# Where the zeros of a graph layer's score table stand in the DMA queue: behind the first value weights, and tied to the last stores of both projections

## The chip, the cores and the metric

The kernel runs on one core of one Trainium2 chip. The metric is the device time of one execution in microseconds. The median of three runs is compared.

## What is computed

The kernel computes two layers over a graph of 625 nodes with 1024 features and 10,000 edges. The change lies in the first of them, which adds two things to x: a graph attention (GATv2) and a linear attention. Cut to what matters:

```python
x = xn * rsqrt(mean(xn**2) + eps) * rms_w            # xn: layer norm of the input
x = x @ W_down                                       # 1024 -> 256
xl, xr = x @ Wl, x @ Wr                              # left and right projection, 625 x 256
msg = xl[src] + xr[dst]                              # one row for each edge (and each self loop)
e = einsum('ehd,hd->eh', leaky_relu(msg), att)       # 4 scores for each edge
p = exp(e - max over dst)                            # softmax over the edges of a destination
out = segment_sum(p / denom * xl[src], dst) @ W_up
# beside it, from the same xn, linear attention with 16 heads:
k, v, q = phi(xn @ W_k + b_k), xn @ W_v + b_v, phi(xn @ W_q + b_q)
```

Then come a quantised feed-forward block, a second layer of graph convolution and linear attention, and an attention with a mixture of eight experts. They take most of the time and are not touched.

## The kernel before, in words

The nodes are tiled as 5 tiles of 125 rows. In the first stage each tile is loaded, normalised (`norm`), transposed (`turn_x`), multiplied by W_down (`down`) and by both projections at once (`left_right`, lines 541 to 551). The result of `left_right` is in SBUF in `xlr`; its left half is stored to the DRAM tensor `xl_d` from ScalarE's queue and its right half to `xr_d` from GpSimd's queue, by the helper `rows_dma` (lines 171 to 174). That helper makes two DMAs of each tile, of 112 and of 13 rows.

The edges are worked on by gathers. 79 chunks of up to 128 edges are grouped by two. For each chunk GpSimd gathers rows of `xl_d` and of `xr_d` (`gather`, line 611), VectorE adds and weighs them into four scores (`score_group`, `score`, lines 586 to 594 and 621), ScalarE takes the exponential into `es`, and GpSimd scatters the result into `table` in DRAM (`scatter`, line 631). `table` has an entry of four values for each pair of nodes, source by destination, and is 128 * 3080 entries of 16 bytes, 6160 KB. An entry without an edge must be zero, so the table is filled with zeros by one DMA from the small tile `none` (line 404) before anything is scattered into it. The scores of the self loops (`own`) go into the table's diagonal from ScalarE's queue (`self_loops`).

Meanwhile TensorE computes the linear attention: `key` and `value` for each tile (`pk` and `pv` in the profile, 16 matmul records each), and between them the counts of the edges by one-hot matmuls (`pct`, line 467, operands in `ring`). After that come `query` and `answer` (`pq`, `pd`, `po`) and the output projection (`mixed`, line 745).

The order in which each engine takes its work is the order in which the program writes it down, in this stage by hand: `manual_schedule` fixes the order of TensorE, VectorE, ScalarE, GpSimd and SyncE. `Stream` (`do`) issues the work of one step's TensorE part and, one step later, the part that evacuates its result. `work(us)` adds planned time to a counter, and when it has passed a threshold, `one_beat` puts one group of edges into the queues: the self loops if due, the scores of an earlier group, its exponentials, then its gathers and the scatters of a still earlier one. The first gather of a group (a beat) is held back until the latest matmul group written down before it is done:

```python
if j == 0 and side == 0 and "pe" in latest:
    behind(got, latest["pe"])
```

`behind(ins, name)` makes one instruction wait for another by a semaphore; nothing else of it runs.

SyncE's queue holds the large loads in this order: the tiles of x with W_down, the projections' weights, the biases of the linear attention, the first key weights (`lin.wk`, two DMAs of 1024 KB, a `Half`), the zeros, the first value weights (`lin.wv`, two DMAs of 1024 KB), and after those the biases and weights of the linear attention's second half. An instruction that waits holds up all that stand behind it in the same engine's queue.

When all scatters are done, GpSimd loads the table back in five parts (`load_table`, `tb`), VectorE multiplies it by the counts (`weigh`, `pT`, line 841), and TensorE sums it (`sums`, `pg`).

Of the kernel before, what the change touches and what calls it, by code (L numbers as in the profile page):

```python
# [20 lines left out]
NT = 5  # L21
P = 125
# [20 lines left out]
def gps_kernel(tc: tile.TileContext, w: dict, out: bass.AP):  # L43

    again = attempt(tc, w, out, False)
    with tc.If(again > 0):
        attempt(tc, w, out, True)  # L50
# [3 lines left out]
def attempt(ctx: ExitStack, tc: tile.TileContext, w: dict, out: bass.AP, shifted: bool):  # L54

    nc = tc.nc
# [6 lines left out]
    def ps1(name):  # L63
        pool, n = psums[-1]
        return pool.tile([128, 512], FP, tag="ps1", name=name, bufs=n)
# [61 lines left out]
    def group(dst, pairs):  # L127

        for i, (lhsT, rhs) in enumerate(pairs):
            made = nc.tensor.matmul(dst, lhsT=lhsT, rhs=rhs, start=(i == 0), stop=(i == len(pairs) - 1))  # L130
        latest["pe"] = made.ins.name
# [3 lines left out]
    def behind(ins, name):  # L135

        tc.add_manual_dep(ins.ins, name, mybir.DependencyInfo(mybir.DependencyClass.Sync,
                                                              mybir.DependencyReason.DATA), reason="pace")
        return ins
# [30 lines left out]

    def rows_dma(eng, dst, src):

        eng.dma_start(out=dst[0:112], in_=src[0:112])
        eng.dma_start(out=dst[112:P], in_=src[112:P])


    graph = ctx.enter_context(ExitStack())
# [41 lines left out]
    def mid(shape, name):  # L219
        return midp.tile(shape, FP, tag="mid", name=name)  # L220
# [135 lines left out]
    with ExitStack() as st0:  # L356
# [4 lines left out]
        table = dram.tile([128 * 3080, 4], FP, name="table")  # L361
# [3 lines left out]
        with ExitStack() as edges:  # L365
# [4 lines left out]

            xin = big.tile([P, NT, D], FP, tag="big", name="xin")
            rows_dma(nc.sync, xin[:, 0, :], xrows[0])

            si = pool.tile([128, EN], I32, name="si")
            di = pool.tile([128, EN], I32, name="di")
            rw = pool.tile([128, KC], FP, name="rw")
            nc.scalar.dma_start(out=rw, in_=w["rms_w"])
            rows_dma(nc.sync, xin[:, 1, :], xrows[1])
            wd = wpool.tile([128, KC, 256], FP, tag="w", name="wd")
            nc.sync.dma_start(out=wd, in_=w["W_down"].rearrange("(k p) n -> p k n", p=128))  # L380
            for t in range(2, NT):
                rows_dma(nc.sync, xin[:, t, :], xrows[t])
# [5 lines left out]
            def load_edges():  # L388
                for dst, name in ((si, "src"), (di, "dst")):
# [8 lines left out]
            none = pool.tile([128, 440], FP, name="none")  # L398
# [2 lines left out]
                                  lambda us: work(us), nc.sync)  # L401
            lin.biases(0)
            lin.wk = Half(wpool, w["L0_Wk"], 0)
            nc.sync.dma_start(out=table.rearrange("(p a b) h -> p a (b h)", p=128, a=28),
                              in_=none.unsqueeze(1).to_broadcast([128, 28, 440]))
            lin.wv = Half(wpool, w["L0_Wv"], 0)
            sf = pool.tile([128, EN], FP, name="sf")
            df = pool.tile([128, EN], FP, name="df")
            up = pool.tile([128, EN], FP, name="up")
# [88 lines left out]
            xlr = mid([P, NT, 512], "xlr")  # L498
            xl_d = dram.tile([N, 256], FP, name="xl_d")
            xr_d = dram.tile([N, 256], FP, name="xr_d")  # L500
# [39 lines left out]
            def left_right(t):  # L540
                def pe():
                    hold["pl", t] = ps1("plr")
                    xdT = hold.pop(("xdT", t))
                    group(hold["pl", t][:P], [(xdT[:, k, :], wlr[:, k, :]) for k in range(2)])

                def after():
                    nc.scalar.activation(xlr[:, t, :], hold.pop(("pl", t))[:P], AF.Identity, scale=r0[:, t:t + 1])
                    rows_dma(nc.scalar, xl_d.rearrange("(t p) e -> t p e", p=P)[t], xlr[:, t, 0:256])
                    rows_dma(nc.gpsimd, xr_d.rearrange("(t p) e -> t p e", p=P)[t], xlr[:, t, 256:512])

                do(None, pe, after)

# [235 lines left out]
            for m in range(KC):  # L788
# [5 lines left out]
                if m < 3:  # L794
# [3 lines left out]
                                      in_=w[("w_gate", "w_up", "w_down")[m]].rearrange("(k p) n -> p k n", p=128))  # L798
# [418 lines left out]
    for m in range(KC):  # L1217
# [8 lines left out]
        a = m % 4  # L1226
# [48 lines left out]
    for b in range(NB_MIN, NB):  # L1275
        nc.gpsimd.dma_start(out=y_d[b * 128:(b + 1) * 128, :].rearrange("p (a n) -> p a n", a=4),
                            in_=zero.unsqueeze(1).to_broadcast([128, 4, 256]))
# [694 lines left out]
```

## Time and profile before

| what | value |
| --- | --- |
| median of 3 runs | 2227.58 us (2226.61 to 2228.72) |
| profiled execution, its own time | 2228.76 us |
| its span, first to last instruction | 2227.0 us |
| mean granted TensorE clock | 0.977 |
| bytes moved by DMA | 301.62 MB, mean 135 GB/s |
| zeros, one DMA | 6160 KB |

A line of a timeline has the start in us, the duration in us, the engine (a q behind it: its queue, an instruction that only issues), the source line, the operation, out<-in by the program's names, the shape, xcount, and in square brackets the idle time of the engine before it with what ended it. "issue" there means that the profile shows nothing it waited for, "remote" that the release came from an event with no instruction beside it in the profile. PE is TensorE, PEld its weight loads, DVE VectorE, ACT ScalarE, POOL GpSimd, SP SyncE. L611 is line 611 of the kernel before.

### The profile page before, as it was taken

How to read it: one execution, taken by the hardware profiler on the slowest of the kernel's cores; microseconds unless marked ns; L12 is line 12 of the kernel's file. 1: busy time of each engine (PE TensorE's matmuls, PEld its weight loads, DVE VectorE, ACT ScalarE, POOL GpSimd, SP SyncE). 2: the span in 40 equal slices, each digit the busy share in tenths (PEclk: the TensorE clock that was granted, in tenths of full speed). 3: DMA queues.
4: the chain of work that ended last, by engine and by line, in shares of the span. 5: the costliest groups of instructions: out<-in, count | busy, mean ns of one | idle time of the engine just before them, and what ended most of it. 6: DMA issues, size and time to landing. Idle time of an engine off the chain costs nothing. (4 is left out here: it accounts for less than half of the span.)

```text
span 2227.0 us, 17363 instructions
## 1 busy us (share of the span) xinstructions
PE 2112.5 (95%) x6934; PEld 1209.9 (54%) x6934; DVE 713.3 (32%) x1214; ACT 194.1 (9%) x354; POOL 341.4 (15%) x349
## 2 busy tenths in 40 slices
PE   8899799578899999999999999999999999999998
PEld 6466375245444777754445767557744444444443
DVE  5765467557623560000113133322011111111112
ACT  2000010001211100000000111100000000000000
POOL 1666656610000020210000000110000000000011
PEclk9999899878999999999999999999999999999999
DMA  9226252071122110231213111021099987997742
GB/s 299 77 62 209 59 182 81 25 212 33 38 85 71 52 38 1 85 142 38 76 38 104 38 38 38 20 103 61 34 347 337 331 325 282 327 331 286 275 144 92
DMA packets 145848, 301.62 MB, mean 135 GB/s; under 512 B 12370, under 2 KB 22436, under 8 KB 145754
## 3 DMA queue, kind: packets, MB, share of 16 engines
q1 hardware_dynamic: 123700, 244.23, 30.7%
q0 software_dynamic: 17376, 46.42, 7.1%
q10 hardware_dynamic: 4678, 9.72, 1.4%
q8 instruction: 58, 0.95, 0.2%
q14 instruction: 36, 0.29, 0.0%
HBM read 277.49 MB, written 22.84 MB: 135 GB/s over the span
## 5 line engine op out<-in xcount | busy, mean ns | idle before, releaser
L130 PE MATMUL pu<-w,xgT 128*128 128x512 f32 x768 | 333.9, 593 | 1.9 <-DVE xgT L1266 1.9
L130 PEld LDWEIGHTS pu<-w,xgT 128*128 128x128 f32 x768 | 144.0, 190 | 174.8 <-issue 171.7
L130 PE MATMUL pyb<-w,hb 128*128 128x512 f32 x384 | 174.3, 599 | 2.5 <-ACT yb L105 2.1
L130 PE MATMUL pq<-xnT,w 128*128 128x313 f32 x512 | 139.6, 432 | 13.8 <-DVE v L286 13.0
L130 PE MATMUL pk<-w,xnT 128*125 128x512 f32 x320 | 143.2, 599 | 3.3 <-issue 2.8
L130 PE MATMUL pv<-w,xnT 128*125 128x512 f32 x320 | 142.2, 597 | 1.5 <-issue 1.1
L130 PE MATMUL p<-tT,w 128*128 128x313 f32 x512 | 136.3, 428 | 0.4 <-DVE tT L1266 0.4
L130 PEld LDWEIGHTS pq<-xnT,w 128*128 128x128 f32 x512 | 98.2, 193 | 53.5 <-DVE v L286 13.8
L130 PEld LDWEIGHTS pyb<-w,hb 128*128 128x128 f32 x384 | 69.8, 189 | 90.9 <-issue 74.8
L1806 DVE TENSOR_TENSOR su<-pu,su 128x512 f32<-128x512 f32 x24 | 16.6, 692 | 314.6 <-ACT su L1805 314.6
L130 PEld LDWEIGHTS p<-tT,w 128*128 128x128 f32 x512 | 96.8, 190 | 37.9 <-issue 1.2
L130 PEld LDWEIGHTS pk<-w,xnT 128*125 128x125 f32 x320 | 59.8, 189 | 77.0 <-issue 76.1
L130 PEld LDWEIGHTS pv<-w,xnT 128*125 128x125 f32 x320 | 59.9, 189 | 75.4 <-issue 72.6
L1789 POOL DMA_INDIRECT xg<-rows_d,slots x12 | 11.4, 946 | 524.8 <-PE pxg L1796 449.0
L631 POOL DMA_INDIRECT table<-es,at x79 | 84.2, 1066 | 49.4 <-issue 26.2
L611 POOL DMA_INDIRECT ga<-xl_d,si x79 | 79.7, 1009 | 74.8 <-issue 33.2
L611 POOL DMA_INDIRECT gb<-xr_d,di x79 | 81.8, 1036 | 25.3 <-issue 22.8
L745 PE MATMUL px<-w,oT 128*125 128x512 f32 x160 | 69.8, 594 | 2.9 <-DVE x L909 2.0
L130 PE MATMUL px<-w,hT 128*125 128x512 f32 x160 | 70.3, 592 | 0.0
L130 PE MATMUL px<-w,oT 128*125 128x512 f32 x160 | 70.3, 592 | 0.0
L130 PE MATMUL ph<-meanT,w 128*128 128x313 f32 x256 | 70.1, 426 | 0.0
L130 PE MATMUL ph<-xnT,w 128*128 128x313 f32 x256 | 70.0, 427 | 0.0
(366 smaller groups left out, 2459.9 us busy)
## 6 DMA issues: line engine op xcount, KB each, us to landing
w<-in_eW_dram SPq DMA_DIRECT2D x144, 1024.0 KB
w<-in_L_Wk_dram SPq DMA_DIRECT2D x8, 1024.0 KB
w<-in_L_Wv_dram SPq DMA_DIRECT2D x8, 1024.0 KB
w<-in_L_Wq_dram SPq DMA_DIRECT2D x8, 1024.0 KB
w<-in_L_Wo_dram SPq DMA_DIRECT2D x8, 1024.0 KB
w<-in_W_self_dram SPq DMA_DIRECT2D x8, 1024.0 KB
w<-in_W_neigh_dram SPq DMA_DIRECT2D x8, 1024.0 KB
w<-in_sW_dram SPq DMA_DIRECT2D x8, 1024.0 KB
```

The costliest lines, as they stand in the source:

```text
L130: made = nc.tensor.matmul(dst, lhsT=lhsT, rhs=rhs, start=(i == 0), stop=(i == len(pairs) - 1))
L611: got = nc.gpsimd.indirect_dma_start(out=ab[g][side][0:p, j, :], out_offset=None, in_=src[:, :], in_offset=bass.IndirectOffsetOnAxis(ap=ix ...
L631: nc.gpsimd.indirect_dma_start(out=table[:, :], out_offset=bass.IndirectOffsetOnAxis(ap=at[0:p, lo + j:lo + j + 1], axis=0), in_=es[0:p, l ...
L745: made = nc.tensor.matmul(hold["px", t][:P, c, :], lhsT=oT[:, k, nodes(t)], rhs=wo[c](k), start=(k == 0), stop=(k == KC - 1 and keep is no ...
L1789: nc.gpsimd.indirect_dma_start(out=xg, out_offset=None, in_=rows_d[:, :], in_offset=bass.IndirectOffsetOnAxis(ap=slots[:, b:b + 1], axis=0))
L1806: nc.vector.tensor_tensor(su, pu[:, 0, :], su, op=ALU.mult)
```

## The change

The zeros' DMA is written down after the two DMAs of the first value weights instead of ahead of them, on the same queue. In addition it now waits for four stores: the two pieces of the last tile's left projection (`xl_d`) and the two of its right projection (`xr_d`). For that, `rows_dma` returns the DMAs that it makes. Nothing else moves: every other instruction keeps its place on its engine, and only the semaphores that the DMAs use are dealt out anew.

```diff
     def rows_dma(eng, dst, src):
-        eng.dma_start(out=dst[0:112], in_=src[0:112])
-        eng.dma_start(out=dst[112:P], in_=src[112:P])
+        return [eng.dma_start(out=dst[lo:hi], in_=src[lo:hi]) for lo, hi in ((0, 112), (112, P))]
...
             lin.wk = Half(wpool, w["L0_Wk"], 0)
-            nc.sync.dma_start(out=table.rearrange("(p a b) h -> p a (b h)", p=128, a=28),
-                              in_=none.unsqueeze(1).to_broadcast([128, 28, 440]))
             lin.wv = Half(wpool, w["L0_Wv"], 0)
+            zeros = nc.sync.dma_start(out=table.rearrange("(p a b) h -> p a (b h)", p=128, a=28),
+                                      in_=none.unsqueeze(1).to_broadcast([128, 28, 440]))
...
                     nc.scalar.activation(xlr[:, t, :], hold.pop(("pl", t))[:P], AF.Identity, scale=r0[:, t:t + 1])
-                    rows_dma(nc.scalar, xl_d.rearrange("(t p) e -> t p e", p=P)[t], xlr[:, t, 0:256])
-                    rows_dma(nc.gpsimd, xr_d.rearrange("(t p) e -> t p e", p=P)[t], xlr[:, t, 256:512])
+                    for put in (rows_dma(nc.scalar, xl_d.rearrange("(t p) e -> t p e", p=P)[t], xlr[:, t, 0:256])
+                                + rows_dma(nc.gpsimd, xr_d.rearrange("(t p) e -> t p e", p=P)[t],
+                                           xlr[:, t, 256:512])):
+                        if t == NT - 1:
+                            behind(zeros, put.ins.name)
```

## The prediction

> **What bounds the kernel now.** I read the page first, then the timelines of each engine from 0 to 140 us, where the change lies, then the waits up to 460 us, then the timelines again around 385 and 454 us, where the edge stage ends. The page says that TensorE is the bound of the whole:
>
> ```profile
> PE 2112.5 (95%) x6934; PEld 1209.9 (54%) x6934; DVE 713.3 (32%) x1214; ACT 194.1 (9%) x354; POOL 341.4 (15%) x349
> ```
>
> So an edit counts only if it moves TensorE. The timeline of SyncE (start, duration, instruction) shows the zeros leaving at 20.84 and the value weights held back behind them until 39.30:
>
> ```profile
> 20.84 0.62 SPq L404 DMA_DIRECT2D table<-none  x1
> 39.30 5.45 SPq L121 DMA_DIRECT2D w<-in_L_Wv_dram  x2
> ```
>
> ScalarE's timeline shows the last store of the left projection; its second piece (13 rows) is 6.3 us behind its first:
>
> ```profile
> 45.93 0.31 ACTq L173 DMA_DIRECT2D xl_d<-xlr  x1
> 52.19 0.31 ACTq L174 DMA_DIRECT2D xl_d<-xlr  x1
> ```
>
> The zeros' packets (1760 bytes, 3584 of them) run in the trace from 28.2 to 51.6 us: this store leaves when they have ended. GpSimd's timeline shows what that delays. In square brackets stand the idle time before an instruction and what ended it:
>
> ```profile
> 57.64 1.36 POOL L611 DMA_INDIRECT ga<-xl_d,si  x1 [10.15 <-issue]
> ...
> 77.62 0.94 POOL L611 DMA_INDIRECT gb<-xr_d,di  x1 [0.30 <-issue]
> 80.91 0.95 POOL L611 DMA_INDIRECT ga<-xl_d,si  x1 [2.35 <-remote]
> ...
> 120.84 0.97 POOL L611 DMA_INDIRECT ga<-xl_d,si  x1 [3.41 <-PE pv L130]
> ```
>
> The first gather waits for all ten pairs of stores and starts at 57.64. From there GpSimd runs without a pause to 78.6, then stands before the fifth group (beat 4, 80.91), whose first gather is tied to a matmul by `behind(got, latest["pe"])`. TensorE in the same stretch:
>
> ```profile
> 45.01 7.03 PE L130 MATMUL pk<-w,xnT 128*125 128x512 f32 x16
> 51.88 4.16 PE L467 MATMUL pct<-ring 128*125 128x313 bf16 x30
> 55.88 7.03 PE L130 MATMUL pv<-w,xnT 128*125 128x512 f32 x16
> 62.74 4.16 PE L467 MATMUL pct<-ring 128*125 128x313 bf16 x30
> 66.75 7.03 PE L130 MATMUL pk<-w,xnT 128*125 128x512 f32 x16
> 73.61 2.56 PE L467 MATMUL pct<-ring 128*125 128x313 bf16 x18
> 77.06 0.29 PE L467 MATMUL pct<-ring 128*125 128x313 bf16 x1 [0.89 <-issue]
> ```
>
> From 25 us to 76 us it runs without a gap: neither weights nor zeros hold it. After 76 us it crawls, one matmul in 0.7 us, though these matmuls wait for no semaphore that is late. VectorE sees the same thing:
>
> ```profile
> 80.67 0.69 DVE L265 TENSOR_TENSOR kb<-pk,bk_t 125x512 f32<-125x512 f32 x1 [5.63 <-remote]
> ```
>
> The last matmul of that `pk` began at 73.18 and its semaphore came at 80.65. Such late completions come again: at 109.7, 157.7, 227.0, 271.5 us. The end of the edge stage is late as well, but there the gathers wait for TensorE and not the other way round:
>
> ```profile
> 384.86 0.96 POOL L611 DMA_INDIRECT ga<-xl_d,si  x1 [8.50 <-PE px L745]
> ```
>
> TensorE then idles 31.66 us until 454.23, waiting for the weighted table (`pT`), which waits for the last scatters and the load of the table.
>
> **What the Trainium skill says.** "DMA: Bandwidth & Descriptors", section "Issuing engines are not separate DMA queues": transfers issued from the scalar, sync and gpsimd engines end on the same 16 DMA engines and interleave. The trace agrees: from 30 to 50 us the mean DMA share is 1.05 at 377 GB/s, and the stores land late inside it. The same page, "Queues, rings and completion order": an engine goes round its queue rows by packets, so a stream is shared and not shut out; from 48 to 52 us the row of SP took 72%, those of ScalarE and GpSimd 18% and 17%, which fits. "Perfetto Trace Analysis", "Summary: the profiler window per engine type": the end of a matmul in a profile is estimated. The trace agrees at 73.8 against 80.65 us, so I go by semaphores there.
>
> **The change, part by part.**
>
> *Value weights ahead of the zeros.* Two DMAs of 1024 KB leave near 21.5 us, not at 39.3 to 44.8. They queue behind the key weights as the zeros did, and `pk` at 45.01 has its weights ahead of them as before. The reader, `pv`, starts at 55.88 right behind the 30 `pct` matmuls with no idle time shown: gain 0. Cover: all TensorE work up to 55.9 us. If they landed no sooner than before, nothing would change either.
>
> *Zeros behind the last stores.* One DMA, 0.62 us on SP's queue. In the queue SP stands at this wait from about 22 to 49 us. Behind it is the second half's key bias, which left at 158.49 us because it waits for VectorE; so the wait holds nobody: 0. No instruction is added on GpSimd or ScalarE; the tie changes SP's waits only.
>
> *Stores without the zeros beside them.* The last are issued at 45.93 to 46.83 us. A small unhindered store, that of `own` at 71.52, landed at 73.5, so I take 2 us: landed near 49. ScalarE loses its 6.6 us stand before the table load for the first exponential; this brings `ke` from 53.82 to about 52.8 (VectorE ends `kb` at 52.8), 1 us, and `kf` with it; TensorE does not wait for either before 170 us: 0.
>
> *First gather.* It also waits for the first `pk`, whose matmuls end near 52.0. So it moves from 57.64 to about 52.4, by 5.2 us, and not by the 8 us that the stores gain. Groups cost 4 x 1.25 us = 5.0 us each, and those from 2 on are tied to matmuls: group 2 to the first `pv` (62.7), group 4 to the second `pk`. GpSimd is level with its ties from group 2 on instead of from group 4. Its later start times are then TensorE's, as at 120.84 and 384.86, so the lead itself is worth 0 at the end.
>
> *Zeros beside gathers.* 6.31 MB from about 51 us. At 377 GB/s less the gathers' 131 KB per 1.25 us = 105 GB/s that is 6.31 / 0.272 = 23 us, to about 74; with the packets taken in turn (1760 against 1024 bytes, 63% of 377 GB/s) 27 us, to 78. The first scatter is at 94.28: covered. The first store of `own` is issued by ScalarE at 71.52 and waits for the zeros: ScalarE stands 3 to 6 us, ahead of an `es` exponential whose scatter is 20 us off, and ahead of `ke` at 81.40: covered by 3 us; without that cover the excess would go to `kf`.
>
> *The stall.* What is left is TensorE's stall at 73 to 81 us. In the trace it ends 2 us after GpSimd has stopped before its tie (78.6, then 80.65), likewise at 271.5 after a stop at 268.6. If GpSimd's unbroken run holds TensorE, a run that begins 5.2 us sooner meets its tie 5.2 us sooner, and TensorE is let go 5.2 us sooner. As all later beats hang on TensorE, this lasts to the end: -5.2 us. The trace does not show the cause, so I bound it: at best the stall goes, and the one at 99 to 110 is halved: windows 70 to 110 us hold 7.65 us of idle TensorE, so -9 with the half clock after it; at worst one stretch more, +7 to +13 (the lateness of `pk` at 73.2 is 7.5, that of `pv` at 258.7 is 12.8). I take -5.2.
>
> Sum: 0 + 0 + 0 + 0 - 5.2 us. Against the profiled execution (2228.76 us, span 2227.0) that gives 2223.6; against the median of 2227.58, 2222.4 us.
>
> **The rivals.**
>
> *A. Nothing moves.* The stall has another cause and stays as it is. For it: every visible reader of the moved transfers has slack, and the last gathers wait for TensorE. Against it: TensorE's loss lies exactly where GpSimd's pattern changes. Time: 2227.6, give or take 3.
>
> *C. Slower.* The late completions come from load on the memory paths, not from GpSimd's run. Then 23 us of zeros laid over the gathers, at 51 to 74 us, bring a stretch more, where before only gathers ran. Place: first `pv` or second `pk`; price 7 to 13 us, so 2235 to 2240; it decides once a semaphore of TensorE comes over 4.5 us later than before. Against it: from 30 to 56 us the same stream ran at full rate and TensorE lost nothing. The delay of `own` belongs here only if the zeros landed after 81 us, below 210 GB/s.
>
> *D.* The gathers still start near 57 us, as one of the stores keeps a shared semaphore with another slow transfer. Then case A's time results.
>
> **How the numbers follow.** A measurement tells about 0.2% (4.5 us) from no change. The stall let go sooner: 0.47, of which 0.38 beyond 0.2%, as -5.2 lies close to the edge; A and D: 0.29; C: 0.24. So faster 0.38, same 0.38, slower 0.24. The likeliest case's own range is 2217 to 2226. The range over all goes from the best bound with a little more, 2216, to 2236, the lower part of C.
>
> **What would show it.** Right: `table<-none` issued near 49 us; first gather near 52.4; second `pk` complete near 75; all later work about 5 us earlier, the gap before `pg` still 31 us. Wrong: first gather at 57; the second `pk`'s semaphore at 80 or later; TensorE gaps between 51 and 74 us; a changed gap before `pg`, which would mean that the end of the edge stage is not tied to TensorE's pace as I read it.

## The result: 7 us faster, and the profile after

| | before | after |
| --- | --- | --- |
| median | 2226.66 us (2223.88 to 2228.72, 6 runs) | 2219.55 us (2218.18 to 2222.72, 6 runs) |
| profiled execution | 2228.76 us | 2218.18 us |
| its span | 2227.0 us | 2216.4 us |
| mean granted clock | 0.977 | 0.978 |

The ratio of the times is 0.9969, with a 95% interval of 0.9956 to 0.9982. The forecast was 2222.4. The program's start was 0.88 us later in the profiled execution of after (first `pk` at 45.89 against 45.01); this has to be taken off every start below.

The page's line of engines shows the same work as before:

```profile
PE 2115.5 (95%) x6934; PEld 1213.3 (55%) x6934; DVE 712.4 (32%) x1214; ACT 193.9 (9%) x354; POOL 339.3 (15%) x349
```

The timelines of SyncE, ScalarE and GpSimd (start, duration, instruction, in brackets the idle time ahead and its end) show that the edit does what it says:

```profile
22.05 3.11 SPq L121 DMA_DIRECT2D w<-in_L_Wv_dram  x2
49.71 0.62 SPq L404 DMA_DIRECT2D table<-none  x1
...
46.81 0.76 ACTq L173 DMA_DIRECT2D xl_d<-xlr  x2
...
53.21 1.02 POOL L613 DMA_INDIRECT ga<-xl_d,si  x1 [4.84 <-PE pk L130]
64.06 0.94 POOL L613 DMA_INDIRECT ga<-xl_d,si  x1 [1.01 <-issue]
76.40 0.94 POOL L613 DMA_INDIRECT ga<-xl_d,si  x1 [2.21 <-PE pct L466]
```

The value weights leave at once, the zeros leave at 49.71, and the two pieces of the last store go out together (x2, 0.76 us) where the second piece used to be 6.3 us behind. The first gather starts 4.43 us sooner, 5.31 less the later start. TensorE in the stretch of the old stall:

```profile
67.63 7.03 PE L130 MATMUL pk<-w,xnT 128*125 128x512 f32 x16
74.49 4.33 PE L466 MATMUL pct<-ring 128*125 128x313 bf16 x30
78.66 7.03 PE L130 MATMUL pv<-w,xnT 128*125 128x512 f32 x16
```

The 30 `pct` matmuls run in one piece. They had been broken up from 76 us on, at 0.7 us a matmul. The comparison of starts on TensorE, before and after, is not a constant shift, however:

| first matmul of | before | after | difference |
| --- | --- | --- | --- |
| second `pk` | 66.75 | 67.63 | +0.88 |
| second `pv` | 81.97 | 78.66 | -3.31 |
| third `pv` | 113.54 | 100.39 | -13.15 |
| last `pv` of the first half | 159.59 | 150.02 | -9.57 |
| first `pq` | 272.33 | 254.70 | -17.63 |
| last `px` ahead of the edge stage's end | 394.86 | 382.87 | -11.99 |
| `pg` | 454.23 | 441.82 | -12.41 |
| end | 2227.0 | 2216.4 | -10.6 |

Two stalls (73 to 81 and 99 to 110 us) are gone. One grew: the counts behind the fifth `pk`, which lost time at 155 to 158 us before, do so at 144 to 150 us now. One is new (265 to 271 us), and a wait of 13.01 us before the first `pq` became 2.21. The end of the edge stage looks as it did:

```profile
441.82 0.68 PE L130 MATMUL pg<-xl,pT 125*125 125x65 f32 x2 [31.23 <-DVE pT L843]
```

Where such stalls are dealt out anew between two traces, their sum says little on a cause. In the runs that follow the kernel before took 2199.2, 2197.6 and 2198.3 us on three chips, where it took 2226.7 us here; the record does not name the chip of this pair. Times are therefore only compared between runs on one chip. Of the kernel before on the first of these chips, two slow runs of 20 (4610 and 9684 us) are left out.

### The profile page after: what moved, and what is told of

It is laid out like the page before. It is cut to its first block, busy times and chain, and to the rows that moved or that the text cites. A ratio compares the mean times of both kernels' runs of the same rounds, so it can differ in the third digit from the quotient of the medians.

```text
span 2216.4 us, 17365 instructions
## 1 busy us (share of the span) xinstructions
PE 2115.5 (95%) x6934; PEld 1213.3 (55%) x6934; DVE 712.4 (32%) x1214; ACT 193.9 (9%) x354; POOL 339.3 (15%) x349
## 5 line engine op out<-in xcount | busy, mean ns | idle before, releaser
L1157 DVE TENSOR_TENSOR z<-pz,z 125x512 fp32r<-125x512 f32 x10 | 6.9, 692 | 196.8 <-ACT z L1155 196.8
```

Of the source, the lines that this page charges most:

```text
L1157: nc.vector.tensor_tensor(low, src, high.bitcast(FP), op=ALU.subtract)
```

## Experiments

The theories at the start: **1**, the prediction's (GpSimd's run holds TensorE, and a run that begins sooner lets it go sooner); **2**, the tie or the place of the zeros matters by itself, not the first gather; **3**, chance (TensorE's stalls fall where they fall). A fourth came out of the first runs: **4**, the chain of gathers and scatters on GpSimd sets the end of the edge stage, and starting it sooner ends it sooner by what later waits leave.

### The changed kernel again, on a chip without stalls

No edit.

> The changed kernel again, to be timed on the same chip as the next ones. Theory 1 (GpSimd's first gather starts earlier, and with that TensorE's stalls fall elsewhere) and theory 2 (the zeros no longer run beside the stores) both expect 6 to 9 us below the kernel before, first gather near 53, no stall of TensorE between 46 and 100 us.

Measured: 2193.81 us (6 runs) against 2199.18; ratio 0.9966 (0.9954 to 0.9979; the two medians alone give 0.9976). So the gain is there, at -5.4 us by the medians. No TensorE stall is: idle time of TensorE between 45 and 350 us that no wait explains comes to 10.6 and 11.4 us in the traces of the first pair, and to none in this trace and all that follow, those of the kernel before included. The step "the stall" of the prediction has nothing to act on there. The stage's end in its timelines of GpSimd and TensorE:

```profile
52.44 1.02 POOL L613 DMA_INDIRECT ga<-xl_d,si  x1 [4.84 <-PE pk L130]
...
348.93 0.96 POOL L613 DMA_INDIRECT ga<-xl_d,si  x1 [2.64 <-PE px L747]
...
358.94 27.71 PE L747 MATMUL px<-w,oT 128*125 128x512 f32 x64
417.90 0.68 PE L130 MATMUL pg<-xl,pT 125*125 125x65 f32 x2 [31.26 <-DVE pT L843]
```

GpSimd's waits before tied gathers come to 3.9 us in all, beyond the 0.30 us that lie between any two of its transfers (the expectations below say 3.75, as a wait of 0.18 us was overlooked). The wait for `px` at 348.93 is 2.3 us of it.

### The order alone, without the tie

```diff
             lin.wk = Half(wpool, w["L0_Wk"], 0)
+            lin.wv = Half(wpool, w["L0_Wv"], 0)
             nc.sync.dma_start(out=table.rearrange("(p a b) h -> p a (b h)", p=128, a=28),
                               in_=none.unsqueeze(1).to_broadcast([128, 28, 440]))
-            lin.wv = Half(wpool, w["L0_Wv"], 0)
```

> The kernel before with the zeros moved behind the first value weights, and without the tie to the stores. Theory 1: the zeros' packets now run from about 33 to 56 us beside the stores; the last piece of the left projection is no longer on the zeros' semaphore, but it shares the DMA engines; first gather at 53 to 57, gain between 0 and 7 us, in step with how early that gather is. Theory 2: the zeros still run beside the stores, so no gain: within 2 us of before. Theory 3 (any small shift deals the stalls out anew): anything from -10 to +10 us with the first gather in no relation to it.

Measured: 2194.15 us (8 runs), 5.0 us under the kernel before; ratio 0.9978 (0.9966 to 0.9991). The zeros left at 28.12 and ran beside the stores, and yet the first gather started at 53.84, not at 56 to 57:

```profile
46.41 0.31 ACTq L173 DMA_DIRECT2D xl_d<-xlr  x1
46.77 0.42 ACTq L174 DMA_DIRECT2D xl_d<-xlr  x1
```

The last store's second piece is not held. In the trace of before this piece and the zeros count on the same semaphore (number 103 in both), and the piece was issued (52.19) only when the last of the zeros had landed (52.17); in this kernel the dealing gives the zeros number 109 and the piece 105. So most of the 5 us come from the semaphore, which the new order happens to free, and the tie is hardly needed for it. What the zeros cost as load can be read as well: the last stores landed 5.3 to 6.3 us after their issue here, 1.6 to 2.3 us in the changed kernel. That agrees with what the Trainium skill says in "DMA: Bandwidth & Descriptors", section "Issuing engines are not separate DMA queues": engines' transfers interleave on the same 16 DMA engines.

### The first gather late, all else as changed

The first gather waits in addition for the matmuls of the first six counts.

```diff
+                    if g == 0 and j == 0 and side == 0:
+                        hold["first"] = got
...
+                        if "first" in hold:
+                            behind(hold.pop("first"), latest["pe"])
```

> The changed kernel with one more wait: the first gather is held until the first six counts are done (about 56.9 us), so that GpSimd starts near 57.3, as in the kernel before, while weights, stores and zeros stay as in the changed kernel. Theory 1: the gain is gone, within 3 us of before (2224 to 2230), and the stall of TensorE at 73 to 81 us is back. Theory 2: the gain stays, 6 us or more below before. Theory 3: some other number, with stalls at other places than in either kernel.

Measured: 2196.11 us (12 runs), ratio 0.9978 (0.9969 to 0.9987); the first gather at 56.76. No stall came at 73 us; as the kernel before has none on such a chip either (below), this does not decide on theory 1. By the medians it is 2.3 us slower than the changed kernel and 3.1 faster than the kernel before, whose first gather came at 57.01 and 56.07 in the traces below. Half of the effect was still unexplained.

### Few gathers and scatters

Only the first five groups are gathered, into buffers that the later groups read again, and only the first is scattered (the last cut).

```diff
-                if j < n:
+                if j < n and g < 5:
...
-                a, b = ab.pop(g)
+                a, b = ab[g % 5]
...
+                    if g > 0:
+                        return
```

> The changed kernel, gathering only the first five groups of edges and scattering only the first; VectorE and ScalarE still work on every group, on stale rows (the output lacks those edges). If GpSimd's indirect transfers cause TensorE's slow stretches, TensorE runs from the first pk to the last px (45.9 to 410.6 us in the changed kernel, 364.7 us long) without them, in about 349 us, its busy time there, and the stretches end after the first five groups. If they have another cause (VectorE's or TensorE's own work), the stretches stay and it takes over 360 us. The gap before pg shrinks in either case, since the last scatters are gone.

The output lacks the edges of all groups but the first. Measured: 2203.57 us, one run; the total is not compared, since what comes after works on other values and has other counts (7046 matmuls where the changed kernel has 6934). What counts is TensorE up to 386 us:

```profile
358.03 27.71 PE L749 MATMUL px<-w,oT 128*125 128x512 f32 x64
385.58 1.20 PE L130 MATMUL pg<-xl,pT 125*125 125x65 f32 x8
```

The last `px` begins 0.9 us sooner than in the changed kernel, the gap before `pg` is gone, and `pg` comes 32.3 us sooner. So on this chip GpSimd's work costs TensorE no more than 0.9 us up to there: the gain is there with nothing for theory 1 to release. And the gap is the wait for the chain of gathers and scatters. This made theory 4.

### The kernel before, traced twice without stalls

No edit in either.

> The kernel before, for a trace from the chip on which the last four ran. Theory 4 (where TensorE has no slow stretches, GpSimd's chain of gathers and scatters is the bound of the edge stage and its first gather sets its end, less the idle time that its ties leave): first gather near 57.5, hardly any idle time before tied gathers, last scatter 2 to 4 us after the 406.0 us of the changed kernel there, pg at 420 to 422 instead of 417.9, TensorE without stall until then. If TensorE's stalls at 73 and 99 us come from the kernel, they are in this trace as well and pg is 10 us or more later.

> The kernel before once more, for a second trace without TensorE's stalls. If a start at 57 us always loses as in e4_before: first gather 57.0 us, last gather 392 to 394, pg near 423. If the loss where the second half's weights are loaded (a scatter of 152.75 us landed 7.3 us later and held the next until 160.85) hangs on the phase in which GpSimd comes there: first gather 57.0 again, but that scatter lands in 2 to 3 us or in 6 or more, and the last gather lies between 389 (as in e2_late_gather) and 394.

Measured: 2198.23 us and 2194.18 us, on two chips, neither of them that of the changed kernel's trace above; the first `pk` of the three traces begins within 0.4 us. Here are first gather and `pg` of the first trace, then of the second:

```profile
57.01 1.07 POOL L611 DMA_INDIRECT ga<-xl_d,si  x1 [9.01 <-issue]
423.50 0.68 PE L130 MATMUL pg<-xl,pT 125*125 125x65 f32 x2 [36.11 <-DVE pT L841]
```

```profile
56.07 1.03 POOL L611 DMA_INDIRECT ga<-xl_d,si  x1 [8.37 <-issue]
419.93 0.68 PE L130 MATMUL pg<-xl,pT 125*125 125x65 f32 x2 [32.49 <-DVE pT L841]
```

With the changed kernel's 417.90 the end of the edge stage comes 5.6 and 2.0 us sooner than here, while the last `px` starts within 0.8 us of the same time in all three (359.68, 359.73, 358.94). In the first trace a single gather waited for a tie, by 0.34 us (217.84); the wait of 8.50 us at 384.86, on which the prediction leant, is one of the stalled trace only.

Why the two differ shows between 150 and 163 us. SyncE sends the second half's weights from 152.86 and 152.47 us on, 1024 KB each at about 390 GB/s, and each scatter waits for the one before to land. Scatters of the first trace in GpSimd's timeline, then those of the second:

```profile
152.75 1.06 POOL L631 DMA_INDIRECT table<-es,at  x1 [0.30 <-issue]
160.85 1.17 POOL L631 DMA_INDIRECT table<-es,at  x1 [4.08 <-DVE ring L446]
```

```profile
150.98 0.99 POOL L631 DMA_INDIRECT table<-es,at  x1 [0.30 <-issue]
155.41 0.99 POOL L631 DMA_INDIRECT table<-es,at  x1 [0.30 <-issue]
161.76 0.98 POOL L631 DMA_INDIRECT table<-es,at  x1 [2.54 <-issue]
```

From issue to landing these take 6.5 to 7.3 us in the first trace and 2.3 to 6.2 in the second. The releaser "ring" in the first is only what ended nearest: the instruction waits for the semaphore of the scatter of 152.75. That one left with the weights and landed after 7.3 us; its counterpart of 150.98 left 1.5 us ahead of them and landed after 2.3 us, and the chain got one more group through before the burst. Gather for gather the two chains were 1.8 us apart ahead of the burst, 5.6 us in it, and 3.8 at the last (393.09 and 389.25). The changed kernel is caught too (152.94, landed 7.1 us later), and its lead over the second trace went from 3.6 us at the first gather to 1.0 behind the burst. It did not stay there: behind the weights that SyncE sends from 256 us on it was 5.8 (gather of 258.96 against 264.78), at 339 us 4.1, and 1.8 from the gather of 348.93 on, whose tie to `px` costs the changed kernel 2.3 us; at `pg` it was 2.0. So the first gather does not set the end alone; what each burst and the last tie do to the chain counts as much.

That the kernel before takes both ways from run to run would fit the scatter of its times: 2191.6 to 2203.7 us in 59 runs on one chip, with the changed kernel at 2191.5 to 2195.6 in 22 runs on the same chip. Which way a run took is known for its trace alone, so this is argued, not shown. The eleven traces without stalls that hold all gathers, those of the later sections included, agree with it. In four of them (order alone with and without ties, the late gather, the second trace here) a scatter left 1.5 us ahead of the first of the weights and landed after 2.2 to 2.3 us, and from the 25th to the 35th gather of `xl_d` it took 48.2 to 48.8 us. In the other seven the scatter nearest to the weights left between 0.1 us ahead of them and 1.8 us behind, landed after 6.3 to 7.3 us, and the same stretch took 49.1 to 51.9 us. No run changes this phase and nothing else. The phase would also account for what the late gather left unexplained, since that kernel's chain ran as the second trace's here (162.19 for the scatter behind the burst, last gather 389.14). Why all of its 12 runs lay within 3.5 us stays open, and with it theory 2 for that half of the effect.

### The first gather ten us later still

It waits for the second set of counts.

```diff
-                        if "first" in hold:
+                        if "first" in hold and f == lin.value:
```

> The changed kernel with its first gather held until the second set of counts is done, near 67 us instead of 53. Theory 4: 14.5 us later, less the 3.75 us of idle time before tied gathers that the changed kernel shows on this chip, so last scatter and pg about 11 us later, 7 to 11 us of it in the total: 2201 to 2205 where the changed kernel takes 2193.8. Theory 1 as predicted (later starts are TensorE's, the lead is worth nothing at the end): pg moves by less than 3 us.

Measured: 2209.8 us (5 runs), ratio 1.0056 (1.0037 to 1.0076), so 12.2 us slower than before. More than was expected. The first gather came at 67.72, the last at 403.48, and `pg` at 434.15:

```profile
374.97 27.71 PE L751 MATMUL px<-w,oT 128*125 128x512 f32 x64
434.15 0.68 PE L130 MATMUL pg<-xl,pT 125*125 125x65 f32 x2 [31.48 <-DVE pT L847]
```

Against the changed kernel's trace, 15.3 us lost at the first gather are 16.3 us lost at `pg`. The slack that I had counted on was eaten because TensorE came late as well (`px` 374.97, 16.0 later). VectorE takes the scores in its fixed order and stood 7.51 us before a late gather (74.49); later it stood 5.01 and 5.66 us for ScalarE, whose stores of `own` waited for late scatters. Behind that VectorE made `ring` late, for which TensorE waited 3.38, 1.54 and 6.08 us between 101 and 122 us. So the first 4.3 us of delay cost 2.0 us at `pg` (417.90 to 419.85, the late gather's), and the next 11 us cost 14.3.

### Ties of the gathers, and the two ways to free the store

Four kernels on one chip: the changed kernel; the changed kernel without the ties of gathers to matmuls; the new order alone, without those ties; the kernel before without them. The one edit of the last three:

```diff
-                    if j == 0 and side == 0 and "pe" in latest:
-                        behind(got, latest["pe"])
```

> The changed kernel without the ties of the gathers to matmuls: GpSimd runs as far ahead as its buffers let it; the zeros keep their tie. First gather near 49.5 instead of 52.4. Theory 4: 3 us from the start and up to 3.75 us of tied idle time, so the last scatter 3 to 6 us sooner than the 406.0 us of the changed kernel on this chip and the total 2 to 6 us below it. If TensorE is held up by GpSimd running on (the reading in the prediction), TensorE shows stalls before 350 us and the total is not below the changed kernel's.

That was its first run, on the chip of the first trace of before: 2191.51 us (17 runs) against 2197.64, ratio 0.9970 (0.9962 to 0.9979).

> The changed kernel once more, beside the next three. Theory 4 (GpSimd's chain of gathers and scatters sets the end of the edge stage; a first gather 4.6 us sooner is worth what the waits of later gathers leave of it): 5 to 8 us under the kernel before, ratio 0.9963 to 0.9977; first gather near 52.4 us, waits of gathers for their ties under 5 us in all. If the gain is a release of TensorE's stall (my prediction's step): no gain here unless this chip's trace of the kernel before shows that stall.

> The changed kernel without the ties of gathers to matmuls. Theory 4: first gather near 49.4, the chain ends 3.3 us sooner than in the changed kernel, so 2 to 3.5 us less than that. Rival (TensorE's order is the bound, gathers only follow): same as the changed kernel within 1 us.

> The kernel before with the zeros behind the value weights, without their tie to the stores and without the gathers' ties to matmuls: zeros then run from about 30 us, beside the last stores. Theory 4 with the view that a shared semaphore and not the load on the DMA engines held the last store: first gather 49.4 to 50.5, time within 1 us of the changed kernel without ties. If the load of the zeros itself delays the stores: first gather 53 or later, time like the changed kernel's or 1 us over.

> The kernel before without the gathers' ties to matmuls. Theory 4: its gathers wait for the stores and not for a tie, and later ones waited for no tie in the second chip's trace of it, so first gather at 57 and time within 1.5 us of the kernel before. Rival (the ties cost by themselves, whatever the zeros do): 2 to 3.5 us less than the kernel before.

| | time, us | runs | ratio to before (2198.25) | first gather | last `px` | `pg` |
| --- | --- | --- | --- | --- | --- | --- |
| changed | 2193.18 | 22 | 0.9978 (0.9972 to 0.9985) | 52.68 | 358.50 | 417.28 |
| changed, no ties | 2191.72 | 14 | 0.9970 (0.9961 to 0.9980) | 49.58 | 358.62 | 415.34 |
| order alone, no ties | 2192.74 | 14 | 0.9975 (0.9966 to 0.9985) | 53.86 | 358.68 | 415.21 |
| before, no ties | 2196.74 | 22 | 0.9996 (0.9988 to 1.0005) | 57.18 | 366.41 | 422.91 |

The gain of the change is there a third time, -5.1 us. Without the gathers' ties it is 1.5 us more by the medians, less than the 2 to 3.5 expected: the chain, freed at 49.58, reaches the burst at 151.62 and is caught as well (7.0 us to landing). The order alone has its first gather at 53.86 with no tie left, so in it the stores' landing and not the tie is the gate; this was the second branch of that expectation. It ends level with the kernel above it at `pg`, though its first gather is 4.3 us later: its scatter of 150.16 left ahead of the burst and landed after 2.3 us, and from 188 us on the gathers of the two kernels lie within 0.2 us of each other. The 3 us of earlier start that the ties cost are thus gone at the burst, and the 2 us at `pg` that their loss brings come from the tie to `px` near 349 us. And the kernel before is not helped by taking the ties away, as theory 4 had it: they cost nothing where the stores come last.

Its last line tells most. The last `px` is 7.9 us later than in the changed kernel. The largest part of it, 4.69 us, arises over three engines: ScalarE's store of `own` leaves at 109.82, when the scatter of 107.60 has landed (109.75); VectorE stands for ScalarE, and TensorE for VectorE's `ring`. The gap before `pg` absorbs the delay:

```profile
110.63 0.21 ACT L598 ACTIVATE es<-es 128x8 f32<-128x8 f32 x1 [9.85 <-issue]
112.05 0.69 DVE L273 SCALAR_TENSOR_TENSOR kf<-ke,kb 125x512 f32<-125x512 f32 x1 [6.82 <-ACT kb L268]
113.37 4.18 PE L467 MATMUL pct<-ring 128*125 128x313 bf16 x15 [4.69 <-DVE ring L446]
...
366.41 27.71 PE L743 MATMUL px<-w,oT 128*125 128x512 f32 x64
422.91 0.68 PE L130 MATMUL pg<-xl,pT 125*125 125x65 f32 x2 [28.79 <-DVE pT L839]
```

TensorE's pace does not set the end of this stage there; GpSimd's chain does: `pg` is 5.6 us behind the changed kernel's, on one chip. The lowest median of all is that of the changed kernel without the gathers' ties, though its interval overlaps with those of the two kernels beside it.

## Why the prediction was right in size and wrong in its reason

1. **Value weights ahead of the zeros, 0.** As forecast: they left at 22.05, and `pv` follows `pk` by 10.87 us in both traces.
2. **The zeros' wait on SyncE, 0.** As forecast: the second half's key bias left at 150.76, a hundred microseconds behind the zeros.
3. **Stores landed near 49.** Those that the trace shows landed from 48.67 to 49.58. ScalarE's stand is gone (`ke` 53.68, 1.0 us sooner when the later start is taken off, as forecast). The reason for that stand I had put down to the packets of the zeros, and named a shared semaphore only in case D. It was the shared semaphore: the order alone frees it while the same packets run.
4. **First gather, -5.2.** 5.3 us when the start is taken off, held by the first `pk` as said.
5. **Zeros beside gathers, covered.** Packets ran from 51.0 to 70.6 us, 19.6 us and not 23 to 27: 322 GB/s, as the gathers left more than the 272 that I allowed. `own` was issued at 73.05, behind their end, so the 3 to 6 us of stand did not arise. No stall came between 51 and 74 us; case C's place stayed empty.
6. **"The lead itself is worth 0 at the end".** This is the step that failed. It was read from two waits of gathers for TensorE (120.84 and 384.86) that exist because TensorE was stalled in that very trace. Without stalls such waits come to 0.34 and 0.57 us in the kernel before and to 3.9 us in the changed one, 2.3 of them at the tie to `px`; the chain's lead is worth 2.0 to 5.6 us at `pg`.
7. **The stall let go 5.2 us sooner.** Not shown by anything. On the chips of the runs it could not be tried, as no kernel stalls there: late gathers bring no stall, and there is none for few gathers to take away. The gain without any stall shows that it is not needed there. In the first pair two stalls vanished and others grew or came, and 12 us at `pg` is neither 5.2 nor a shift kept from 81 us on. That the median moved by 7.1, close to the sum, is luck: the right number from the wrong term. Where nothing stalls, the same 5 us of earlier gathers are worth about 5 us by another path. What share of the first pair's 7.1 us is this path and what is stalls falling elsewhere, no run tells.

Of the signs I had named, the first four held (zeros at 49, gather at 52.4, second `pk` read by VectorE at 76.43 or 75.5 without the later start, the gap still 31 us). The fifth, all later work 5 us earlier, did not. "A changed gap before `pg`" was to mean that the edge stage's end is not tied to TensorE: in the stalled pair the gap stayed (31.66, 31.23), without stalls it went from 36.1 or 32.5 to 31.3.

## What to carry to other kernels

When a store leaves late, look whether its semaphore is shared with a big transfer before blaming the bandwidth: moving one line may deal the semaphores anew and do most of the work, as the order alone did here (5.0 of 5.4 us). A gap that is equally long in two traces does not say which of its two ends is the cause; take one engine's work away (here, most gathers) and see which end moves. And waits read in a disturbed trace show the disturbance: before a wait is used as cover, look for the same wait in a second trace.

## What the hardware showed that I had not expected

- In the first pair TensorE had stretches in which matmuls of the same shape came 0.7 or 1.4 us apart, with no wait in the profile, and semaphores 7.5 to 12.8 us behind a matmul's begin. Windows of TensorE's busy time, for the kernel before in the first pair and then in its first trace without stalls:

```profile
73.00:81.00 8.00, 5.32 (x29) 3.52 (x28) 2.31 (x6) 0.00 (x0) 4.44 (x6) 0.99 0.29 89
99.00:110.00 11.00, 6.03 (x15) 2.33 (x15) 7.11 (x19) 0.62 (x3) 6.26 (x7) 0.76 0.19 51
```

```profile
73.00:81.00 8.00, 8.00 (x41) 5.67 (x40) 7.16 (x20) 1.32 (x3) 6.17 (x7) 1.00 0.34 101
99.00:110.00 11.00, 9.93 (x40) 5.72 (x38) 5.24 (x14) 1.36 (x3) 6.52 (x7) 1.00 0.22 62
```

  The columns are the window, its length, the busy time of PE, PEld, DVE, ACT and POOL with their instructions, the granted clock, the share of DMA and its GB/s. The first window has 29 matmul records instead of 41 at a granted clock of 0.99, so that clock does not explain it; in the second window it was 0.76. The kernel before was some 28 us longer there than on three other chips, and all of it lies ahead of `pg`: from there to the end it takes 1772.8 us in that trace and 1772.9 in the other. The cause is open; no run has one kernel on one chip in both conditions.
- A chain of small scatters that each wait for the last to land pays 2.1 to 2.3 us for most links alone and 5 to 7 us beside a stream of weights at 390 GB/s. Two runs of one kernel, in which the stream caught different links, differ by 3.6 us at `pg`.
- From 560 to 595 us the granted clock differs from trace to trace (0.76 to 1.00 in windows of 12 and 14 us), and of the changed kernel's two traces without stalls the one lost some 3 us to the other there. Leads at `pg` are therefore not read off the end of a single run.
